# Graph gathers of a four-layer GNN stack as 64-row products on the two halves of TensorE's array

## The chip, the cores and the metric

One core of a Trainium2 chip runs the whole program. The metric is the device time of one execution in microseconds, lower is better. The granted clock is the share of TensorE's full clock that its throttle let through, averaged over a stretch. Ratios are the mean time of one kernel's fast runs over that of the other's fast runs of the same rounds, so they are not quite the ratio of the medians quoted beside them.

## The reference

128 graphs of 64 nodes with 256 features each pass through four layers; after each layer the input is added and normalised. All is fp32. What matters here is how often features are multiplied by an adjacency matrix:

```python
# layer 1: out = norm_adj @ (x @ W) + b
# layer 2: three powers of adj_norm, applied to x @ W.T       (the kernel folds them into one matrix)
# layer 3, five steps:
A = (adj != 0).astype(x.dtype)
for l in range(5):
    m = einsum('bnd,de->bne', h, weight[l])
    agg = einsum('bij,bid->bjd', A, m)         # a gather over each graph's 64 nodes
    h = _gru_cell(agg, h, w_ih, w_hh, b_ih, b_hh)
```

Layer 0 works on subsets of nodes and is not touched by the change.

## The kernel before

Eight graphs form a chunk, and two graphs always lie together on the 128 partitions, so a chunk has `NP` = 4 pairs. An adjacency of 64x64 is spread into a block-diagonal matrix of 128x128 for a pair, half of it zeros. A gather multiplies the features of a pair (stationary, 128 rows of nodes, 128 columns of features) by that matrix (moving):

```python
def gather(src, m, name, tag="ag"):
    a = work.tile([128, 2, NP * 128], F32, tag=tag, ...)
    for k in range(2):                       # two halves of the features
        p = psum("pa")                       # one bank of PSUM, the memory that TensorE writes to
        for q in range(NP):
            nc.tensor.matmul(p[:, q*128:(q+1)*128], src[:, q, k*128:(k+1)*128], m[:, q, :],
                             start=True, stop=True)
        nc.scalar.copy(a[:, k, :], p)
    return a
```

`mid` (layers 1 and 2 of a chunk) calls it twice, with `AT1` and with the folded polynomial `poly`; `messages` calls it once in each of the five steps of the last layer. That is 16 x 7 = 112 gathers. `psum` hands out three rotating banks. The last layer alternates between two chunks. Its gate products use Strassen's scheme, seven products in place of eight (`rz(1)` ... `n(7)`), and the mids of the next chunks are slipped in between as filler. TensorE's program order is fixed by hand:

```python
x.rz(3)
if w:
    w.close()          # w.messages(): the gather of the other chunk
    ...
x.n(6)                 # gate product 6; ScalarE then copies its bank
x.n(5)
next(filler, None)     # a piece of a mid, if one is left
x.n(7)                 # adds onto product 6's bank, after that copy
```

## Time and profile before

| | before |
|---|---|
| median of the first three runs | 2464.16 us |
| TensorE busy with products | 2281.0 us, 93% |
| ... with weight loads | 1994.1 us, 81% |
| VectorE / ScalarE busy | 53% / 44% |
| a gather, first product to next product | 1.78 us |

The lines behind the table are in the prediction. Two readings matter. TensorE is busy almost throughout, so what a change adds to its stream is added to the time. And its busy sums overlap, so durations of single products do not add up: the cost of a group is the distance from its first start to the start of what follows.

### The profile page before, as it was taken

Reading aid. Unit: us, or ns where it says so; the run is one execution under the profiler, and the core shown is the slowest. Engines: PE = TensorE matmul, PEld = TensorE weight load, DVE = VectorE, ACT = ScalarE, POOL = GpSimd, SP = SyncE. Lnnn points to the kernel's source line nnn. Section 1 sums busy time; section 2 is a strip of 40 time slices with the busy share of each in tenths; the row PEclk is TensorE's granted clock in tenths of the full one; section 3 lists DMA queues with packets and bytes.
Section 4 is the critical chain, followed back from the end, with each engine's and each line's share of the span. In section 5 each row is a group of like instructions: output and inputs, shape, how many; then the busy total and the mean of one; then the engine's idle time right before and its main releaser. Section 6 shows DMA issues by size and latency. Waiting matters only on the chain.

```text
span 2462.4 us, 31767 instructions
## 1 busy us (share of the span) xinstructions
PE 2281.0 (93%) x12288; PEld 1994.1 (81%) x12288; DVE 1315.6 (53%) x2914; ACT 1090.6 (44%) x2102; POOL 567.0 (23%) x606
## 2 busy tenths in 40 slices
PE   2999994999999999999999999999999999999996
PEld 2878783788888888888888888888888888888885
DVE  1333324555566556655565556555655565555445
ACT  1343441444444444444445444545454545454443
POOL 1101002322222222222222222222132222222221
PEclk9999996999999999999999999999999999999998
DMA  5222113000000000000000000000000000000000
GB/s 157 67 79 88 50 44 116 3 3 1 3 18 20 1 3 18 20 1 3 18 20 1 3 18 20 1 3 16 22 1 1 9 18 1 1 3 16 1 1 17
DMA packets 55318, 54.34 MB, mean 22 GB/s; under 512 B 24224, under 2 KB 48512, under 8 KB 55168
## 3 DMA queue, kind: packets, MB, share of 16 engines
q1 hardware_dynamic: 51616, 43.74, 5.6%
q0 software_dynamic: 1504, 5.51, 0.6%
q10 hardware_dynamic: 2048, 3.06, 0.4%
q8 instruction: 97, 1.59, 0.3%
q14 instruction: 53, 0.43, 0.1%
HBM read 35.52 MB, written 16.78 MB: 21 GB/s over the span
## 4 chain that ended last, share of the span: by engine, by line
PE 53%; DVE 29%; ACT 9%; POOL 3%; issue 3%; DMA 2%; SPq 1%; DVEq 0%; POOLq 0%; ACTq 0%
PE parz L460 9%; PE pan L460 6%; PE pa L496 6%; PE ps L289 5%; PE pdrz L460 4%; PE pbrz L460 4%; DVE RZ L653 4%; DVE RZ L654 4%; PE ph L274 4%; DVE hn L655 3%; DVE NI L647 2%; DVE NI L648 2%; ACT NI L652 2%; DVE RZ L482 2%; PE pbn L460 2%
## 5 line engine op out<-in xcount | busy, mean ns | idle before, releaser
L476 ACT COPY c<-parz 128x512 f32<-128x512 f32 x240 | 140.4, 585 | 369.9 <-PE parz L460 369.9
L460 PE MATMUL parz<-Th,WHH 128*128 128x256 f32 x960 | 285.9, 379 | 0.0
L460 PE MATMUL parz<-Ta,V 128*128 128x256 f32 x960 | 285.5, 379 | 0.0
L440 POOL TENSOR_TENSOR Th<-hn 128x512 f32<-128x512 f32 x64 | 93.5, 1461 | 653.5 <-DVE hn L655 653.5
L652 ACT ACTIVATE NI<-NI,bih 128x512 f32<-128x512 f32 x160 | 115.5, 722 | 224.4 <-DVE NI L648 224.4
L460 PEld LDWEIGHTS parz<-Ta,V 128*128 128x128 f32 x960 | 182.4, 190 | 24.8
L476 ACT COPY c<-pan 128x512 f32<-128x512 f32 x240 | 141.0, 587 | 125.9 <-PE pan L460 125.1
L440 POOL TENSOR_TENSOR Ta<-agg 128x512 f32<-128x512 f32 x80 | 101.5, 1269 | 400.8 <-ACT agg L499 400.8
L460 PEld LDWEIGHTS parz<-Th,WHH 128*128 128x128 f32 x960 | 176.0, 190 | 21.2 <-ACT c L476 0.5
L478 DVE TENSOR_TENSOR NI<-pdn,c 128x512 f32<-128x512 f32 x80 | 54.8, 684 | 229.8 <-ACT c L476 229.8
L460 PE MATMUL pan<-Ta,V 128*128 128x256 f32 x480 | 147.4, 389 | 20.9 <-ACT c L476 19.7
L625 ACT ACTIVATE RZ<-RZ,brz 128x512 f32<-128x512 f32 x160 | 106.4, 712 | 128.0 <-DVE RZ L488 128.0
L107 POOL TENSOR_TENSOR rs<-ve,mhalf 128x4 f32<-128x4 f32 x64 | 64.5, 1008 | 413.6 <-DVE ve L105 401.7
L460 PE MATMUL pan<-Th,WHH 128*128 128x256 f32 x480 | 143.7, 381 | 0.0
L482 DVE TENSOR_TENSOR NI<-pbn,c 128x512 f32<-128x512 f32 x80 | 55.3, 692 | 149.9 <-PE pbn L460 149.4
L496 PEld LDWEIGHTS pa<-A,h 128*128 128x128 f32 x1024 | 123.7, 192 | 13.9 <-ACT h L669 11.0
L113 ACT ACTIVATE xt<-xt,nb,rs 128x256 f32<-128x256 f32 x192 | 99.7, 589 | 75.3 <-DVE nb L110 75.3
L496 PE MATMUL pa<-A,h 128*128 128x128 f32 x1024 | 125.5, 276 | 7.7 <-ACT h L669 7.6
L289 PE MATMUL ps<-W,hg 128*100 128x256 f32 (+3 forms) x576 | 131.8, 381 | 0.0
L596 PE MATMUL pT<-ident,hn 128*128 128x128 f32 x640 | 96.5, 277 | 25.9 <-DVE hn L655 25.9
L596 PEld LDWEIGHTS pT<-ident,hn 128*128 128x128 f32 x640 | 74.2, 141 | 48.5 <-PE pT L596 34.3
L289 PEld LDWEIGHTS ps<-W,hg 128*100 128x100 f32 (+3 forms) x576 | 91.0, 163 | 27.2
(183 smaller groups left out, 5214.4 us busy)
## 6 DMA issues: line engine op xcount, KB each, us to landing
xt<-in_x_dram SPq DMA_DIRECT2D x16, 512.0 KB
x<-xt SPq DMA_DIRECT2D x16, 512.0 KB
xt<-x SPq DMA_DIRECT2D x16, 512.0 KB
out_dram<-xt SPq DMA_DIRECT2D x16, 512.0 KB
xg<-in_x_dram SPq DMA_DIRECT2D x32, 100.0 KB
W<-in_w_dram POOLq DMA_DIRECT2D x5, 512.0 KB, 9.2
W<-in_w_dram ACTq DMA_DIRECT2D x5, 512.0 KB
a<-in_adj_dram SPq DMA_DIRECT2D x16, 128.0 KB
```

The source lines that it names most:

```text
L113: nc.scalar.activation(y[:, p, :], y[:, p, :], AF.Identity, bias=nb[:, p : p + 1], scale=rs[:, p : p + 1])
L274: nc.tensor.matmul(p, W1[:, g, k, e * 128 : (e + 1) * 128], ag0[:, k, o : o + w], start=k == 0, stop=k == 1)
L289: nc.tensor.matmul(p[:r, h, :], hg[:, e, TOFF[t] - o : TOFF[t] - o + r], W2[:, g, e, :], start=e == 0, stop=e == 3,)
L440: nc.gpsimd.tensor_sub(t[:, 0:2, :], a[:, :, H:], a[:, 0, :].rearrange("p (s n) -> p s n", s=2))
L460: nc.tensor.matmul(bank[:, g, :], w[:, q, i - 1, :], rhs, start=i in (1, 2, 5) and g == 0 and m == 0, stop=m == len(side) - 1, skip_group_ ...
L476: nc.scalar.copy(c, self.a)
L482: nc.vector.tensor_add(C[:, :, 0, :H], b, self.copies.pop(1))
L496: nc.tensor.matmul(p[:, q * 128 : (q + 1) * 128], src[:, q, k * 128 : (k + 1) * 128], m[:, q, :], start=True, stop=True)
L596: nc.tensor.transpose(p[:, q * 128 : (q + 1) * 128], src(q, k), ident)
L625: nc.scalar.activation(RZ[:, q, 0, :], RZ[:, q, 0, :], AF.Sigmoid, bias=b[0])
L652: nc.scalar.activation(n, n, AF.Tanh, bias=bih[:, 4 + j : 5 + j])
L653: nc.vector.tensor_sub(d, self.hT[:, j, :], n)
```

## The change

The intent is to stop multiplying the zero blocks. Each graph gets its own product of 64 rows. The two graphs of a pair lie on different halves of the array's rows, and their products are to run side by side, each into a bank of its own:

```diff
+    halves = [(slice(64 * b, 64 * b + 64), b) for b in range(2)]
     def gather(src, m, name, tag="ag"):
         a = work.tile([128, 2, NP * 128], F32, ...)
+        ps = [psum("pa").rearrange("p (k q n) -> p k q n", k=2, q=NP) for _ in halves]
         for k in range(2):
-            p = psum("pa")
             for q in range(NP):
-                nc.tensor.matmul(p[:, q*128:(q+1)*128], src[:, q, k*128:(k+1)*128], m[:, q, :], ...)
-            nc.scalar.copy(a[:, k, :], p)
+                for f, b in halves:
+                    nc.tensor.matmul(ps[b][:, k, q, :], src[f, q, k*128:(k+1)*128], m[f, q, :], ...)
+        for _, b in halves:
+            nc.scalar.copy(a.rearrange(...)[:, :, :, b, :], ps[b])
@@ the matrices shrink to [128, NP, 64] @@
-        nc.vector.tensor_scalar(A01, Ab, 0.0, None, op0=ALU.not_equal)
+        nc.vector.tensor_scalar(A01, a64, 0.0, None, op0=ALU.not_equal)
-        nc.vector.tensor_mul(AT1, p, dinv1[...])
+        for f, b in halves:
+            nc.vector.tensor_mul(AT1[f], p[f, :, b * N : (b + 1) * N], dinv1[f, ...])
@@ the last polynomial matrix likewise, in two instructions @@
```

More of the change, by code (lines that the diff above doesn't have):

```diff
@@ L488, in product @@
                     nc.vector.tensor_add(C[:, :, 0, H:], self.d, self.copies.pop(6))
+    halves = [(slice(64 * b, 64 * b + 64), b) for b in range(2)]
     def gather(src, m, name, tag="ag"):
         a = work.tile([128, 2, NP * 128], F32, tag=tag, name=name, bufs=2 if tag == "agg" else 1)
+        ps = [psum("pa").rearrange("p (k q n) -> p k q n", k=2, q=NP) for _ in halves]
         for k in range(2):
-            p = psum("pa")
             for q in range(NP):
-                nc.tensor.matmul(
-                    p[:, q * 128 : (q + 1) * 128], src[:, q, k * 128 : (k + 1) * 128], m[:, q, :], start=True, stop=True
-                )
-            nc.scalar.copy(a[:, k, :], p)
+                for f, b in halves:
+                    nc.tensor.matmul(
+                        ps[b][:, k, q, :], src[f, q, k * 128 : (k + 1) * 128], m[f, q, :], start=True, stop=True
+                    )
+        for _, b in halves:
+            nc.scalar.copy(a.rearrange("p k (q b n) -> p k q b n", q=NP, b=2)[:, :, :, b, :], ps[b])
         return a
@@ L514, in mid @@
         )
-        A01 = work.tile([128, NP, 128], F32, name="A01", bufs=4)
-        nc.vector.tensor_scalar(A01, Ab, 0.0, None, op0=ALU.not_equal)
+        A01 = work.tile([128, NP, N], F32, name="A01", bufs=4)
+        nc.vector.tensor_scalar(A01, a64, 0.0, None, op0=ALU.not_equal)
         rsum = small.tile([128, NP], F32, name="rsum")
@@ L529, in mid @@
         yield
-        AT1 = work.tile([128, NP, 128], F32, name="AT1", bufs=1)
+        AT1 = work.tile([128, NP, N], F32, name="AT1", bufs=1)
         p = psum("pT1").rearrange("p (q n) -> p q n", q=NP)
@@ L535, in mid @@
             nc.tensor.transpose(p[:, q, :], A1[:, q, :], ident)
-        nc.vector.tensor_mul(AT1, p, dinv1[:, :, None].to_broadcast([128, NP, 128]))
+        for f, b in halves:
+            nc.vector.tensor_mul(AT1[f], p[f, :, b * N : (b + 1) * N], dinv1[f, :, None].to_broadcast([64, NP, N]))
         poly = work.tile([128, NP, 128], F32, tag="poly", name="poly3", bufs=2)
@@ L550, in mid @@
                 nc.tensor.matmul(p[:, q, :], Ab[:, q, :], poly[:, q, :], start=True, stop=True)
-            poly = work.tile([128, NP, 128], F32, tag="poly", name=f"poly{k}", bufs=2)
-            nc.vector.tensor_add(poly, p, cI[:, k, None, :].to_broadcast([128, NP, 128]))
+            if k:
+                poly = work.tile([128, NP, 128], F32, tag="poly", name=f"poly{k}", bufs=2)
+                nc.vector.tensor_add(poly, p, cI[:, k, None, :].to_broadcast([128, NP, 128]))
+                continue
+            poly = work.tile([128, NP, N], F32, name="poly0", bufs=1)
+            for f, b in halves:
+                n = slice(b * N, (b + 1) * N)
+                nc.vector.tensor_add(poly[f], p[f, :, n], cI[f, k, None, n].to_broadcast([64, NP, N]))
         yield
```

## The prediction

> **What bounds the kernel now.** I read the page's engine totals first, then busy time in windows, then the order of work on TensorE within one step of the last layer, then the gathers' buffers.
>
> ```profile
> PE 2281.0 (93%) x12288; PEld 1994.1 (81%) x12288; DVE 1315.6 (53%) x2914; ACT 1090.6 (44%) x2102; POOL 567.0 (23%) x606
> ```
>
> TensorE is the engine to look at: 93% busy with products, 81% with weight loads, and the next engine, VectorE, at 53%. From 500 us on it is steadier still:
>
> ```profile
> 500.00:1000.00 500.00, 481.78 (x2559) 425.48 (x2558) 295.89 (x606) 236.31 (x435) 127.79 (x135) 1.00 0.03 9
> 1000.00:1500.00 500.00, 481.73 (x2556) 425.35 (x2555) 295.84 (x607) 235.74 (x434) 130.51 (x138) 1.00 0.03 11
> ```
>
> (Columns: window, its length, busy us and count of PE, PEld, DVE, ACT, POOL, then granted clock, DMA share, GB/s.) PE is busy 482 of 500 us at a clock of 1.00, so a nanosecond added to or taken off TensorE's instruction stream there is added to or taken off the time, unless a wait steps in. The busy sums overlap (products are pipelined), so cost must come from spacing. The list in order of time gives it:
>
> ```profile
> 1016.38 0.59 PE L460 MATMUL pdrz<-agg,V 128*128 128x256 f32 x2
> 1016.81 1.95 PE L496 MATMUL pa<-A,h 128*128 128x128 f32 x16
> 1018.59 0.60 PE L460 MATMUL pan<-Ta,V 128*128 128x256 f32 x2
> 1019.03 0.59 PE L460 MATMUL pan<-Th,WHH 128*128 128x256 f32 x2
> ...
> 1020.32 1.95 PE L496 MATMUL pa<-AT,xt 128*128 128x128 f32 x16
> 1022.11 1.06 PE L550 MATMUL pp<-poly,Ab 128*128 128x128 f32 x8
> ```
>
> (Start, length, engine, line, operation, shapes, count.) One gather is 8 products in the source and 16 records: each fp32 product leaves two load-and-multiply passes. It takes 1018.59 - 1016.81 = 1.78 us, 111 ns a pass. A gate product of 256 columns takes 0.43 us for two passes, 216 ns each, about 0.84 ns a moving column. By that rate a 128-column pass should stream in 108 ns. So is a gather pass bound by its columns or by its weight load? Layer 0 has passes with fewer columns and decides it:
>
> ```profile
> 167.90 1.01 PE L306 MATMUL po<-AT,s 72*128 72x72 f32 x8
> 168.75 1.97 PE L274 MATMUL ph<-ag,W 128*128 128x96 f32 x16
> ...
> 186.04 1.03 PE L239 MATMUL pT<-ident,A 112*112 112x112 f32 x9
> ```
>
> Eight passes of 72 rows and 72 moving columns under 128 weight columns last 1.01 us; less the 0.228 us of the last one, (1.01 - 0.228)/7 = 112 ns apart, although 72 columns would stream in 61 ns. Sixteen of 96 columns: (1.97 - 0.25)/15 = 115 ns. Nine transposes whose stationary side is 112 wide: (1.03 - 0.26)/8 = 96 ns. So neither a fixed issue cost nor the moving columns set the 112 ns: the 128 stationary columns do, and 72 rows load no faster than 128. This is the hinge of the prediction: the change halves moving columns and rows, which do not bind, keeps 128 stationary columns, which do, and doubles the passes.
>
> **What the Trainium skill says.** "TensorE: Matmul & The Clock Gate", section "LDWEIGHTS (loading the stationary operand)": a load takes P/1.2 ns with P the columns, whatever the rows: 107 ns for 128. The 112 and 96 ns above agree. "TensorEngine Tiling (Array Packing)", section "Key Properties": tiles of different rows can load and multiply in parallel, and a change of tiling mode drains TensorE. No record here has 64 rows or fewer, so the trace before shows neither. The same page, "Gotcha 1: PSUM Pressure": different row tiles may not write one PSUM bank at once; that is why the change opens two banks for a gather, one for each half.
>
> **The change part by part.**
>
> Gathers. Each mid (layers 1 and 2) has two and each of the five steps of the last layer one, for 16 chunks: 16 x 7 = 112 gathers. Before: 112 x 16 passes x 112 ns = 201 us, 8% of the span. After: 32 passes of 64 rows, 128 stationary and 64 moving columns; 64 columns stream in 54 ns. Three outcomes for the spacing:
> - Loads of the two halves take turns: 32 x 112 ns = 3.58 us a gather, +1.79 us, x 112 = +201 us.
> - Loads of the two halves run beside each other. The order is A first pass, A second pass, B first, B second; with products in order and loads drawn ahead, A's second overlaps B's first and B's second the next A's first. Two passes then take one load time: 16 x 112 ns = 1.79 us, 0 us gained.
> - Loads of 64 rows beside each other and also twice as fast: 16 x 56 ns, -0.9 us a gather, -100 us. Against it: 72 rows gained nothing.
>
> Mode changes. Every gather stands between 128-row products, so 224 changes. No trace duration for a drain; an estimate from this one: a 256-column pass is recorded as 379 ns, and a load starts 0.22 us before its product. If the load may not start until the previous pass is out, starts are 0.38 + 0.22 = 0.60 us apart instead of 0.216 at the entry, +0.38. At the exit a 64-column pass would be recorded as about 223 ns (275 and 379 ns for 128 and 256, the same slope): 0.22 + 0.22 = 0.44 instead of 0.112, +0.33. That is 0.71 us a gather, 80 us in all if the drain is complete, 0 if switching rows is free. I take 40.
>
> Evacuation. Two ACT copies of 128x512 a gather as before (578 ns median), but both now wait for the end of the gather, where the first could start at half time. In the last layer this changes nothing:
>
> ```profile
> who waited for it (us, times):
>   POOL Ta L440: 400.8, 78
>   ACT ag L499: 41.4, 56
>   ACT ag L255: 21.0, 32
>   DVE A L516: 6.6, 6
>   PEld pT L541: 3.4, 6
>   PE pT L541: 1.9, 6
>   ACT agg L499: 1.2, 4
> ```
>
> (Those who waited for the gathers' bank.) The 160 copies of messages waited for PE only 4 times, 1.2 us: ACT reaches them late anyway, held by the sigmoids of the step before. The 56 waits of the mid's copies are followed by work one filler slot later, some microseconds. I count 0.
>
> VectorE. A01 shrinks from 128x512 to 128x256 (427 ns, perhaps 250): 16 x -0.18 = -3 us. The scalings of AT1 and the last poly become two instructions on 64 partitions each: 690 ns becomes about 2 x 430 (half-width forms of the gate work take 420 to 480), 32 x +0.17 = +5 us. On an engine 53% busy: 0. Poly's sharing buffer goes to a single one, which its one use a mid does not contest. Transposes, the other poly products and the gate products stay.
>
> Sum for the middle outcome: 0 + 40 = +40 us, 2504 us.
>
> **Rivals.**
> 1. Loads take turns. For it: one load at a time is all the trace shows, and all products so far used all rows. Against: the skill's page has tiles load independently. Time: 2464 + 201 = 2665, with drains 2705 to 2745.
> 2. Loads are parallel, drain negligible: 2464, within 0.5%. The extra instructions (1792 more of each kind) cost no issue time if they go out twice in 112 ns.
> 3. The intended gain: half the work of each gather really disappears, because the zero blocks are no longer multiplied. Time: 2464 - 100 + up to 80 of drains, 2365 to 2445. Part of the gain would be lost to the recurrence from VectorE through the transposes (PE waited for hn 67 times, 25.9 us in all), because shorter gathers let TensorE reach it sooner.
> 4. A PSUM wait: the gather needs two of three buffers at once. The poly product behind a mid's gather takes the third, and the next waits for VectorE's poly anyway (0.88 us idle before it now). At most 16 x 0.5 = 8 us.
>
> **Range and chances.** I give the parallel loads 50% (2464 to 2545 by the drain), turns 35% (2665 to 2745), the gain 15% (2365 to 2445). The median of that mixture lies in the upper half of the first, 2520 us. Eight in ten: 2430 to 2715. Two per cent are 2415 and 2513. Faster takes most of the third outcome, 0.12; slower takes all of the second and 40% of the first, 0.55; within 2% the rest, 0.33.
>
> **What would show it.** In the list by time, a message gather should have 32 records of 64x64 and, from its first product to the next gate product, take about 1.8 us plus a drain (parallel), 3.6 (turns) or 0.9 (gain). Starts of A and B passes in pairs a few nanoseconds apart mean parallel; even gaps of 112 ns mean turns. A gap at the entry and the exit of each gather, about 0.3 us beyond the usual 0.2, is the drain. ACT's waits for the message bank should stay near zero and VectorE's busy time within 10 us of 1316. What makes me wrong: passes closer than 56 ns on average, a gather slower than 3.6 us, or new waits of PE on ACT.

## The result, and the profile after

The changed kernel takes 2498.52 us (median of 4 runs, 2496.71 to 2500.49) against 2463.8 us before. The ratio is 1.0142, with a 95% interval of 1.0125 to 1.016: 35 us slower, inside 2%.

The engines' line of the page after has 1792 more product records, and nothing else moves much; VectorE gains 2.2 us:

```profile
PE 2323.3 (93%) x14080; PEld 1999.1 (80%) x14080; DVE 1317.8 (53%) x2946; ACT 1089.8 (44%) x2102; POOL 560.5 (22%) x606
```

This is the list in order of time around one message gather after, on TensorE (start, length, line, operation, shapes, count). It answers to the list that the prediction shows of before:

```profile
1031.27 0.59 PE L460 MATMUL pdrz<-agg,V 128*128 128x256 f32 x2
1031.79 2.00 PE L499 MATMUL pa<-A,h 64*128 64x64 f32 x32
1033.72 0.70 PE L460 MATMUL pan<-Ta,V 128*128 128x256 f32 x2
1034.26 0.59 PE L460 MATMUL pan<-Th,WHH 128*128 128x256 f32 x2
```

A pass is one load with its product; each fp32 product in the source leaves two. There are 32 passes instead of 16, yet the gather takes 1033.72 - 1031.79 = 1.93 us, not 3.6. From the last gate product ahead of it to the second one behind it, before took 1019.03 - 1016.38 = 2.65 us and after takes 1034.26 - 1031.27 = 2.99: +0.34 us. The medians over the 78 message gathers that stand between gate products are the same, 2.65 and 2.99. The extra sits at the edges. Gate products are 0.43 us apart; the first pass of the gather now comes 0.52 after the one ahead (+0.09). The gate product behind is 0.70 long instead of 0.59 and is followed after 0.54 (+0.11), and the gather itself is 0.15 longer at its first and last pair.

That the halves run side by side can be read from a narrow window of the same list, cut after the first passes, and of its weight loads:

```profile
1031.27 0.59 PE L460 MATMUL pdrz<-agg,V 128*128 128x256 f32 x2
1031.79 0.33 PE L499 MATMUL pa<-A,h 64*128 64x64 f32 x2
```

```profile
1031.79 0.19 PEld L499 LDWEIGHTS pa<-A,h 64*128 64x128 f32 x2 [0.33 <-issue]
```

Two passes are over in 0.33 us although the first alone is recorded as 0.32 (the longest of its group), and two loads in 0.19 us although one takes 0.188. Two of each start within 0.01 us; in the packed trace the two passes of a pair start 7 ns apart and the pairs 112 ns apart. The 0.33 us of idle load unit ahead of them, put down to "issue", is the way into the 64-row products.

112 gathers x 0.34 us is 38 us. That is already close to the 35 measured, but the experiments show that the agreement hides two smaller terms of opposite sign.

### The profile page after: what moved, and what is told of

It is laid out like the page before. It is cut to its first block, busy times and chain, and to the rows that moved or that the text cites. A ratio compares the mean times of both kernels' runs of the same rounds, so it can differ in the third digit from the quotient of the medians.

```text
span 2494.9 us, 35392 instructions
## 1 busy us (share of the span) xinstructions
PE 2323.3 (93%) x14080; PEld 1999.1 (80%) x14080; DVE 1317.8 (53%) x2946; ACT 1089.8 (44%) x2102; POOL 560.5 (22%) x606
## 4 chain that ended last, share of the span: by engine, by line
PE 55%; DVE 28%; ACT 7%; POOL 4%; issue 3%; DMA 2%; SPq 1%; POOLq 0%; DVEq 0%; ACTq 0%
PE parz L460 9%; PE pa L499 8%; PE pan L460 7%; PE ps L289 5%; PE pdrz L460 4%; PE pbrz L460 4%; DVE RZ L665 4%; PE ph L274 4%; DVE RZ L664 4%; DVE hn L666 3%; DVE NI L658 2%; PE pdn L460 2%; DVE RZ L482 2%; PE pbn L460 2%; ACT xt L113 2%
## 5 line engine op out<-in xcount | busy, mean ns | idle before, releaser
L440 POOL TENSOR_TENSOR Th<-hn 128x512 f32<-128x512 f32 x64 | 88.5, 1382 | 758.4 <-DVE hn L666 652.8
L460 PE MATMUL pan<-Ta,V 128*128 128x256 f32 x480 | 156.4, 407 | 17.2 <-ACT c L476 16.9
L499 PEld LDWEIGHTS pa<-A,h 64*128 64x128 f32 x2048 | 119.3, 188 | 25.5 <-issue 18.6
L499 PE MATMUL pa<-A,h 64*128 64x64 f32 x2048 | 128.1, 275 | 3.7 <-ACT h L680 3.7
```

Of the source, the lines that this page charges most:

```text
L440: nc.gpsimd.tensor_sub(t[:, 0:2, :], a[:, :, H:], a[:, 0, :].rearrange("p (s n) -> p s n", s=2))
L460: nc.tensor.matmul(bank[:, g, :], w[:, q, i - 1, :], rhs, start=i in (1, 2, 5) and g == 0 and m == 0, stop=m == len(side) - 1, skip_group_ ...
L499: nc.tensor.matmul(ps[b][:, k, q, :], src[f, q, k * 128 : (k + 1) * 128], m[f, q, :], start=True, stop=True)
```

## The experiments

Ten kernels ran. All gave correct results.

| kernel | median us | ratio to before (95%) |
|---|---|---|
| before (beside the first four) | 2463.49 | |
| halves in turn | 2727.05 | 1.1075 (1.1058 to 1.1091) |
| split gather | 2511.70 | 1.0196 (1.018 to 1.0211) |
| split gather, in the kernel before | 2457.34 | 0.9975 (0.9959 to 0.9992) |
| quarters | 2442.12 | 0.9911 (0.9896 to 0.9925) |
| before (beside the next four) | 2465.45 | |
| messages only | 2480.00 | 1.0063 (1.005 to 1.0077) |
| mids only | 2485.52 | 1.0079 (1.0066 to 1.0093) |
| quarters, product 6 first | 2412.18 | 0.9784 (0.977 to 0.9797) |
| before, product 6 first | 2447.44 | 0.9927 (0.9914 to 0.9941) |
| before (beside the last two) | 2465.63 | |
| first mids only | 2474.26 | 1.004 (1.0023 to 1.0057) |
| later mids only | 2474.22 | 1.0036 (1.0021 to 1.0052) |

The theory under test: the body of a gather costs the same as before, because two halves share each load time, and the loss is the passage in and out, 0.34 us each. The main rivals: 64-row loads are simply twice as fast and nothing is parallel; or the loss comes from the later copies, or from the gathers of layers 1 and 2.

### Halves in turn

```diff
-        for k in range(2):
-            for q in range(NP):
-                for f, b in halves:
+        for f, b in halves:
+            for k in range(2):
+                for q in range(NP):
```

> The changed kernel, but each gather does all eight products of rows 0-63 first and then all eight of rows 64-127 (same products, same banks, same copies). Theory (the two halves' loads and products run beside each other only when they are neighbours in program order): no pairs left, 32 passes at 112 ns = 3.58 us a gather, +1.79 us x 112 = about +200 us over the changed kernel, 2700 us. Rival (loads of 64 rows are simply twice as fast, or TensorE reorders the halves by itself): no more than 10 us over the changed kernel's 2498 us.

It took 2727 us, 228 more than the changed kernel. The list by time:

```profile
1021.79 0.59 PE L460 MATMUL pdrz<-agg,V 128*128 128x256 f32 x2
1022.32 3.39 PE L499 MATMUL pa<-A,h 64*128 64x64 f32 x32
1025.64 0.70 PE L460 MATMUL pan<-Ta,V 128*128 128x256 f32 x2
```

The same 32 passes now take 1025.64 - 1022.32 = 3.32 us. So 64-row loads are not faster by themselves, and neighbours in program order are what makes the halves overlap. The rival with fast loads is out. 3.32 is a little under 32 x 0.112 = 3.58: at the seam between the halves a few passes did overlap. The lengthening explains (3.32 - 1.93) x 112 = 156 us. The expectation of 200 is missed on both sides: the gather is shorter than I assumed, and something else costs 72 us more. The windows of the two kernels show what it is (window, its length, busy us and count of each engine, and then, third from the end, the granted clock):

```profile
1000.00:1500.00 500.00, 489.37 (x2673) 426.94 (x2672) 264.75 (x555) 214.05 (x389) 115.23 (x125) 0.96 0.03 10
```

```profile
1000.00:1500.00 500.00, 484.36 (x2972) 418.87 (x2971) 290.59 (x606) 233.38 (x430) 126.42 (x136) 1.00 0.03 10
```

The first is the halves in turn, the second the changed kernel. TensorE is recorded as 98% busy in the first, yet its clock was 0.96; over the whole run it was 0.946 against 0.984. Lost clock, 2724.7 x 0.054 - 2494.9 x 0.016 = 107 us, is more than enough for the 72; some of it fell where TensorE waited anyway.

The packed trace shows where. Its clock record has only full and half clock, in windows of 3.4 us. Of these windows between 549 and 2440 us, 39 ran at full clock and held 27 to 32 passes of the gathers: each was followed by a window at half clock. Another 463 ran at full clock and held 0 to 26 such passes: none was. At half clock, gate passes stand 427 ns apart instead of 216. That happened 291 times in the last layer, against 7 in the changed kernel, and adds some 57 of the 72 us. A likely reason, not tested: by 0.84 ns a column, the 64 columns of a pass stream for only an estimated 54 of its 112 ns, and the recorded busy time, made of overlapping records of 272 ns, does not show that.

### Split gather, and its control

```diff
         for k in range(2):
             for q in range(NP): ...
+            if k == 0 and between:
+                between()              # gate product 6, x.n(6), which followed the gather
```

> The changed kernel, with each of the 80 message gathers cut in two: the products of the first feature half, then the gate product number 6 of the other chunk (which followed the whole gather), then the second feature half. The same instructions, but one more passage from 128-row to 64-row products and back for each message gather. Theory (each passage in and out costs about 0.33 us of TensorE time): 80 x 0.33 = +27 us over the changed kernel, 2525 us. Rival (the 35 us come from the later copies or from waits for buffers, not from the passages): within 8 us of the changed kernel's 2498 us.

> The control: the same cut of the message gathers in the kernel before, where all products have 128 rows. Both theories: within 5 us of the kernel before, 2464 us, unless the moved gate product brings a wait of its own, which would then have to be taken off the cost of the other cut.

The split took 2511.7 us, 13 more than the changed kernel, and the control took 6 us less than the kernel before, just outside the 5 expected. Relative to its control the extra 80 passages cost 13 + 6 = 19 us, 0.24 us each: between the two expectations, nearer to the theory's. One second passage looks like the first:

```profile
1013.45 0.59 PE L460 MATMUL pdrz<-agg,V 128*128 128x256 f32 x2
1013.98 1.11 PE L499 MATMUL pa<-A,xt 64*128 64x64 f32 x16
1015.02 0.70 PE L460 MATMUL pan<-Ta,V 128*128 128x256 f32 x2
1015.55 0.59 PE L460 MATMUL pan<-Th,WHH 128*128 128x256 f32 x2
1016.08 1.11 PE L499 MATMUL pa<-A,xt 64*128 64x64 f32 x16
1017.12 0.70 PE L460 MATMUL pdn<-Ta,V 128*128 128x256 f32 x2
```

Each half gather takes 1.04 us, so two take 2.08 where one whole gather takes 1.93; each is entered 0.53 after a gate product and followed by a gate product of 0.70. The missing part is a wait that disappeared. Here are the waits of TensorE for the ScalarE copy behind product 6 (total us, times, longest) in the kernel before, in the changed kernel, in the split one and in the split control:

```profile
PE pan L460 <- ACT c L476: 19.7, 16, 3.3
```

```profile
PE pan L460 <- ACT c L476: 16.9, 16, 3.3
```

```profile
PE pan L460 <- ACT c L476: 4.1, 2, 3.3
```

```profile
PE pan L460 <- ACT c L476: 14.0, 10, 3.3
```

The split kernel shed 13 us of that wait, the control 6. With both corrected, an extra passage costs (13 + 13) / 80 = 0.33 us (the control's 6 us gain and the 6 us it shed cancel), which is close to the edge cost read from the list. The correction rests on one trace of each kernel and was made after the result; without it the figure is 0.24. This run also showed that the order of product 6 and the gather was worth something by itself.

### Messages only, mids only

Both forms of `gather` side by side, the 64-row form called from one place only:

```diff
-        ag = gather(xt, AT1, "ag1")          # messages only: the old form here, and for poly
+        ag = gather_full(xt, AT1, "ag1")
```

> The changed kernel with the 64-row form for the 80 message gathers of the last layer alone; the 32 gathers of layers 1 and 2 and their matrices as before. Theory (0.34 us a gather for going in and out of the 64-row products, everything else of a gather the same): 80 x 0.34 = +27 us over the kernel before, 2491 us. Rival (the cost sits in the gathers of layers 1 and 2, whose copies now come later and whose scalings are two instructions): within 5 us of the kernel before.

> The complement: the 64-row form for the 32 gathers of layers 1 and 2 alone, the messages as before. Theory: 32 x 0.34 = +11 us over the kernel before, 2475 us; with the run of the messages alone it adds up to the +35 us of the whole change. Rival (the cost sits here): +25 us or more.

They cost 15 and 20 us: the sum is that of the whole change, but the shares are not the expected 27 and 11. To find where, I read in each trace when the first and last product `parz<-Th` of the last layer started; the distance is the stretch of the gate products, and the first number is the length of the start (group, count, shortest/median/longest ns, first and last start). Before, after, messages only, mids only:

```profile
L460 PE MATMUL parz<-Th,WHH x960: 379/379/483, 488.3 to 2429.2; 128*128 128x256 f32 x192
```

```profile
L460 PE MATMUL parz<-Th,WHH x960: 379/379/483, 495.9 to 2462.6; 128*128 128x256 f32 x192
```

```profile
L460 PE MATMUL parz<-Th,WHH x960: 379/379/483, 487.0 to 2445.5; 128*128 128x256 f32 x192
```

```profile
L460 PE MATMUL parz<-Th,WHH x960: 379/379/458, 500.9 to 2451.7; 128*128 128x256 f32 x192
```

The stretch is 1940.9, 1966.7, 1958.5 and 1950.8 us: +25.8 for the whole change, +17.6 for messages, +9.9 for mids. The mids' 28 gathers in that stretch at 0.34 would be 9.5: as expected. The start is 488.3, 495.9, 487.0 and 500.9: +7.6 and +12.6 where the first two chunks' mids have the new form, none where they have not. (One trace each: the split control, whose start is that of the kernel before, began at 492.8.) Messages, at 78 x 0.34 = 26.5, cost 9 less than expected. The traces show where, in two parts. Adding up in the trace the time from product 5's last pass to product 7's first, in the 24 places with no filler between, gives 27.4 us before and 21.0 after. TensorE used to wait there for the copy behind product 6, and the longer gather now fills 6.4 us of it. The rest lies at the entry of the gathers: TensorE's waits there for ScalarE's copy of `h` were 7.6 us in the kernel before and 4.3 with messages only, 3.3 less. Together that is the 9 us.

### The start: first mids only, later mids only

The 64-row form by chunk, in the gathers of layers 1 and 2 alone:

```diff
+        half = c < 2          # first mids only; later mids only: c >= 2
+        gat = gather_half if half else gather
```

> The 64-row form for the four gathers of layers 1 and 2 of the first two chunks alone, which run between 380 and 490 us with no gate products beside them; all else as in the kernel before. The run with all 32 such gathers cost 20 us where 32 x 0.34 = 11 were expected, and in its trace 12.6 us of that lay before the first gate product, with a granted clock of 0.71 between 380 and 490 us against 0.80. Theory (the start with little TensorE work is what pays, through the clock): +6 to +13 us over the kernel before, with a lower clock in that stretch. Rival (the low clock there was that run's own chance, the passages alone count): 4 x 0.34 = +1 us, within 4 us of the kernel before.

> The complement: the 28 gathers of layers 1 and 2 of all later chunks, which stand among gate products. Passages alone: 28 x 0.34 = +9.4 us over the kernel before under both theories, 2473 us, with the first gate product where the kernel before has it. If it is +17 us or more, the start was not the cause and each such gather costs about 0.6 us.

Both cost about 9 us. Four gathers at the start cost as much as 28 later ones. The windows from 380 to 490 us, before and with the first mids only:

```profile
380.00:490.00 110.00, 73.04 (x369) 64.67 (x370) 57.17 (x183) 32.23 (x88) 34.70 (x48) 0.80 0.19 66
```

```profile
380.00:490.00 110.00, 73.57 (x370) 63.53 (x371) 57.38 (x186) 27.47 (x80) 26.57 (x38) 0.72 0.19 66
```

The granted clock there falls from 0.80 to 0.72, and 110 x 0.08 = 9 us of full clock is what is lost; the gate stretch of that run is 2438.7 - 497.8 = 1940.9 us, the same as before, and the later mids only start their gate products at 486.9. So the start pays. That it pays through the clock can be read from products that the change leaves alone: between 370 and 500 us the 216 passes of `pf`, `pd` and `pp` were busy for 47.8 us before and 57.2 here, +9.3, while those of the gathers took 0.6 more. It is not one run's chance either: in the five kernels whose first mids have the 64-row form with 128 columns the clock from 380 to 490 us was 0.70 to 0.75, in the five with the old form 0.77 to 0.82.

Why the 64-row form lowers the clock there is not shown: TensorE works there with long gaps in both kernels. Passes that stream for half of their time, as with the halves in turn, are one candidate. Another is a new stall: the second chunk's first gather halts after two passes until VectorE has emptied the bank that it needs second (0.7 us in the trace of the changed kernel).

### Quarters, and product 6 first

If a gather is bound by the load of 128 stationary columns, then halving the columns as well should gain. Each product becomes four, on the four quarters of the array:

```diff
-    nc.tensor.matmul(ps[b][:, k, q, :], src[f, q, k*128:(k+1)*128], m[f, q, :], ...)
+    for j in range(2):
+        e = k * 128 + 64 * j
+        nc.tensor.matmul(ps[b][64*j:64*j+64, k, q, :], src[f, q, e:e+64], m[f, q, :], ...)
```

> The changed kernel, with the 128 stationary columns of each product also cut in two, so that four products of 64 rows by 64 columns stand on the four quarters of the array. Theory (a gather is bound by the load of 128 stationary columns, 112 ns a pair of passes, and loads on different quarters run beside each other): 16 x 56 ns = 0.9 us a gather instead of 1.79, -0.9 x 112 = -100 us, about 2400 us, the passage costs staying. First rival (quarters of the same rows take turns): 2498 us or a little more. Second rival (load and product of one quarter do not overlap, 56 ns each at 128 columns, so 28 + 56 = 84 ns): 16 x 84 = 1.34 us, -50 us, 2448 us.

It ran in 2442.12 us, less than both kernels, by 0.9% and 2.3%. The list by time:

```profile
1009.77 0.59 PE L460 MATMUL pdrz<-agg,V 128*128 128x256 f32 x2
1010.29 1.16 PE L501 MATMUL pa<-A,h 64*64 64x64 f32 x64
1011.38 0.70 PE L460 MATMUL pan<-Ta,V 128*128 128x256 f32 x2
1011.92 0.59 PE L460 MATMUL pan<-Th,WHH 128*128 128x256 f32 x2
```

64 passes take 1.09 us, edges included, against 1.93 for 32 passes of 128 columns. So the stationary columns did set the 112 ns, and four quarters overlap as two halves do. The same edges remain (0.52 ahead, 0.70 behind). (1.93 - 1.09) x 112 = 94 us should have come out, as the theory said, but 56 did; the second rival's number, 2448, is nearer to the time, but its spacing (1.34 us a gather) is not what the trace shows. Half of the missing 38 us, 36.2 - 16.9 = 19, is again the wait for the copy behind product 6:

```profile
PE pan L460 <- ACT c L476: 36.2, 36, 3.3
```

The copy stands in ScalarE's queue behind the two copies of the gather, and the gather no longer covers it. The cure is to give that product its place ahead of the gather:

```diff
             x.rz(3)
+            x.n(6)
             if w:
                 w.close()
                 ...
-            x.n(6)
             x.n(5)
```

> The quarter form, with the gate product number 6 of the other chunk moved from behind the message gather to before it. The quarter form's gather became 0.84 us shorter than that of the changed kernel (94 us in all) but only 56 us came out, and TensorE's waits for the ScalarE copy behind product 6 grew from 17 to 36 us. Theory (the shorter gather uncovered that copy, which stands in ScalarE's queue behind the two copies of the gather): the wait nearly vanishes, -30 us, about 2412 us. Rival (the missing gain is lost to the granted clock or elsewhere): no change beyond the 6 us that the move brought in the kernel before, 2436 us.

> The control: the same move in the kernel before. It had 19.7 us of waits for that copy. Both theories: -5 to -18 us, 2446 to 2459 us.

Both times came out as expected, the control at the edge of its range. The quarters with product 6 first take 2412.18 us, 2.2% below the kernel before, the one version here that is faster by more than 2%. Its wait fell to 12.5 us, a third of what it was, and did not nearly vanish. The move alone gives the kernel before 18 us; the quarters then give 35 more. By the spacing it should have been (2.65 - 2.15) x 112 = 56, and no run here shows where the other 21 went; in the one trace of each, 5 of them lie ahead of the first `parz<-Th` (490.5 and 495.1). So the idea behind the change was worth having once the columns were cut too.

## Why the prediction was right or wrong

The range held the result, and "within 2%" came true, though I had given "slower by over 2%" more (0.55 against 0.33). The point of 2520 was a hedge between outcomes; the middle outcome by itself was 2504, 5 us off.

- **The hinge: stationary columns bound a gather, and halves share the load time.** Right. The body went from 1.78 to 1.93 us, edges included, for twice the passes. The quarters confirmed the bound, halves in turn that it is sharing. One detail was off: I described A's second pass overlapping B's first; the trace has two passes starting together from the first one on. Two readings were loose: the 112-wide transposes also move 112 columns (an estimated 94 ns), so alone they do not single out the stationary side, the 72- and 96-column passes do; and not all earlier products used all rows, since layer 0 has 72 to 112.
- **Mode changes, 40 us taken out of 0 to 80.** The size was right: 0.34 us a gather, 38 us. Its parts were not: I put 0.38 at the entry and 0.33 at the exit for a full drain and then halved the sum without a reason from the trace. The entry cost 0.09, the rest, 0.25, lies in the first and last passes and in the first gate product behind. That 40 fitted was luck.
- **Every gather costs the same.** This was the unspoken step, and it failed. Messages cost 15 us instead of 27, since they filled waits that were already there; the four gathers at the start cost 9 instead of 1, with a lower granted clock. The two errors nearly cancelled.
- **Evacuation, 0.** Right for the changed kernel: the wait for product 6's copy did not grow (19.7 to 16.9 us). It held only while the gather stayed long; the quarters uncovered it. My third rival had looked for the loss of such a gain in the recurrence through the transposes; TensorE's wait for `hn` was 25.9 us before and 27.1 in the quarters, so it was not there.
- **VectorE, 0.** Right: +2.2 us, predicted +2.
- **The rivals.** Loads in turn at 2665 to 2745: halves in turn came to 2727, but by another sum: 156 us of passes and 72 of which most is lost clock. The intended gain did not occur in this form. The PSUM wait of up to 8 us hardly showed: TensorE's wait for the second poly product is 14.0 us before and after, and the gathers' own new wait for a bank comes once, 0.7 us, in the stretch before the gate products.

## What to carry to other kernels

Before cutting a product to fit its data, find which of its sides sets the spacing: here it was the stationary columns, so halving rows and moving columns gained nothing, while halving the stationary columns too gained 0.84 us a gather. Put products for different parts of the array next to each other in program order, in bursts as long as the order allows, since each passage in and out cost 0.34 us. When a burst gets shorter, look at once for the copy that it used to hide.

## What the Trainium skill lacked or had wrong

- "TensorEngine Tiling (Array Packing)". "Key Properties" says that a change of tiling mode drains TensorE and gives no cost. Here going into 64-row products and back cost 0.34 us among gate products (0.33 by the split gather). "Theoretical Speedup" promises up to 2x for a dimension of 64 or less; it does not say that row halves gain nothing where the load of 128 stationary columns sets the pace: 1.78 us a gather became 1.93. (Against the same 32 passes in turn, 3.32 us, the pairs did gain 1.7 times; the comparison that counts here is with one zero-padded product.) Halves of rows and columns together gave 1.09.
- "TensorE: Matmul & The Clock Gate", Part 3, says in one line that a load overlaps products in flight only when their rows differ, although it allows a background weight buffer some lines above. In the kernel before, passes of the same 128 rows stood 112 ns apart, though 128 columns alone take about 108 ns to stream by the gate products' rate: load and product overlap there too. The part says that products keep their order, but has no figure for what separating two tiles' products costs. Eight products of one half ahead of eight of the other lost nearly all the overlap: 3.32 us instead of 1.93.
- The same page, Part 1, ties the half clock to how busy TensorE has been, and says only of transposes, in Part 4, that they do not count as busy in the same way. With the halves in turn the clock was 0.96 in a window in which TensorE was recorded as 98% busy, and every full-clock window of 3.4 us with 27 or more of their passes was followed by one at half clock (39 of 39, against 0 of 463 others).
